# Local deformable attention: spread and write a step later, GpSimd's hat work on other steps, the first head's weights by three products and one sum

## The chip, the cores and the metric
The kernel runs on one core of a Trainium2 chip. The metric is the device time of one execution in microseconds (us), as a median over runs. The engines are TensorE (PE; its weight loads are shown as PEld), VectorE (DVE), ScalarE (ACT), GpSimd (POOL) and SyncE (SP), which issues most DMA transfers. Each works through its own queue in order.

## The reference
The program is a chain of four layers, each a token mixer and a feed-forward part, on x of (4, 64, 64, 128). The change touches the first mixer alone, a deformable attention with 4 heads of 32 channels and 9 taps (3x3, dilation 1, 3, 5, 7 for heads 0 to 3):

```python
qkv = conv2d(qkv.transpose(0, 3, 1, 2), w_dw, padding=1, groups=3 * c) + b_dw[None, :, None, None]
mask = jax.nn.sigmoid(conv1x1(pconv(q_img, pconv_mask_w), w_mask, b_mask))
for i in range(G):
    off = conv1x1(pconv(q_img, pconv_off_w[i]), w_off[i], b_off[i])
    dil = 2 * i + 1
    k_list.append(deform_sample(kv[0, :, i], off, mask, dil, dil * PAD))
    v_list.append(deform_sample(kv[1, :, i], off, mask, dil, dil * PAD))
...
attn = jax.nn.softmax(jnp.einsum('bgnc,bgckn->bgnk', qf, ks_), axis=-1)
out = jnp.einsum('bgnk,bgckn->bgnc', attn, vs_)
out = out.transpose(0, 2, 1, 3).reshape(b, h, w, c)
return out @ w_proj + b_proj
```

`deform_sample` reads the image at each tap moved by an offset, with bilinear weights between four pixels. Where no offset is over 1 in size, as with these inputs, a tap touches pixels of a small neighbourhood only.

## The kernel before, in words
`deformable_project` computes q, k, v, offsets and mask and leaves them in HBM. `deformable_near` is the local part, where the change lies. It works on 128 tiles of 128 pixels (two image rows); a tile's turn is a **step** T, and four tiles are a **chunk** c with the steps 4c to 4c+3. For each step:
- `products`: GpSimd copies the queries of the tile of the next step into qm (two buffers; L737).
- `product`: 64 TensorE matmuls (L766) give the products of the queries with whole runs of key pixels, in PSUM tiles S, one per head and one buffer each. `copy_products`: ScalarE copies them to `band` (L776). The next product can write S only after that.

For each chunk:
- `hats`, `rows_of_hats` and `hat_products`, all on GpSimd, make the bilinear weights: hat (L697 to L701), hy (L708 to L716), and H, four products for the four heads (L724).
- `attention`, on VectorE: shifts the bands by predicated copies (L785), multiplies them with H (L787), sums to the 9 logits (L794) and subtracts the maximum (L802 to L804).
- `spread`: the exponential on ScalarE (L810), its normalisation (L811 to L813), then the weight of each pixel of the neighbourhood, A, on VectorE: heads 1 to 3 by three products each (L817). Taps of head 0 overlap, so it has one product t0 (L823) and then three copies and additions per tap row (L827 to L830). `write`: four DMAs bring A to HBM (L835).

LAG steps after its product, each tile comes back. `read_dense` reads A in another layout into `dense` (L844), two steps ahead; `transpose` turns it on TensorE (L878), with copies dt to SBUF on ScalarE (L880); `weigh` multiplies it with values (L898; `value_block`, L856, loads them). After every fourth tile ScalarE copies the output to oT (L910, `values_done`), and a step later `projection` does the product with w_proj (L919), a ScalarE copy to o (L921) and two additions on GpSimd (L922, L923).

The order: the loop over T emits the work of a step; `step(T, first, do, 4)` emits `do(c)` at T = 4c + first. The blocks of TensorE (transpose, product, projection, weigh, in this order in a step) are chained by hand, `block`. GpSimd's hat work is tied by hand behind the qm copy of its step, `tc.issue_after(after[0].ins)`. All else is put into the queues by a planner at build time: it goes through the program with its own costs, and an engine that it finds free gets the earliest emitted instruction that it finds ready. Semaphores then keep data in order on the chip, whatever the times are.

Tile pools have a fixed number of buffers by tag: lg, m, me, H and band two; prod, hat, hy, t0, o and oT one; pt (for transposes and projection together) three.

Of the kernel before, what the change touches and what calls it, by code (L numbers as in the profile page):

```python
# [10 lines left out]
F32 = mybir.dt.float32  # L11
I32 = mybir.dt.int32
AF = mybir.ActivationFunctionType
ALU = mybir.AluOpType
AX = mybir.AxisListType
# [345 lines left out]
def window(ap, off, dims):  # L361

    return bass.AP(ap.tensor, ap.offset + off, [list(ap.ap[0])] + dims)
# [245 lines left out]
def deformable_near(k, dr, x, y, qd, kd, vd, od, masks, w_proj, b_proj):  # L609
# [19 lines left out]
    nc, tc = k.nc, k.tc  # L629
# [5 lines left out]
    with ExitStack() as ctx:  # L635
        wp = ctx.enter_context(tc.tile_pool(name="dn_w", bufs=1))
        sm = ctx.enter_context(tc.tile_pool(name="dn_s", bufs=2))
# [18 lines left out]
        for i in range(2):  # L656
            As.append([wp.tile([128, 4, WB[g], 4, 3], F32, tag=f"A{i}{g}", name=f"A{i}{g}") for g in range(4)])
            for t in As[i]:
                nc.vector.memset(t, 0.0)

        dd = [[dr.tile([128, 4 * PP[g] + 12], F32, tag=f"dd{i}{g}", name=f"dd{i}{g}") for g in range(4)] for i in range(3)]

# [14 lines left out]
        def behind():  # L677

            return tc.issue_after(last[0].ins) if last[0] is not None else ExitStack()

        def block(do, *args):

            with behind():
                last[0] = do(*args)
# [6 lines left out]
        def hats(c):  # L691

            of = ofs[c]
            hat = hat_of[c] = sm.tile([128, 8, 3, 4, 3, 3], F32, tag="hat", name="hat", bufs=1)
            src = window(of, 0, [[81, 4], [9, 8], [3, 3], [1, 3]])
            part = lambda i: window(hat, i, [[9, 4], [108, 8], [36, 3], [3, 3]])
            nc.gpsimd.tensor_scalar(part(0), src, -1.0, 0.0, op0=ALU.mult, op1=ALU.max)  # L697
            nc.gpsimd.tensor_scalar(part(2), src, 0.0, None, op0=ALU.max)
            flat = hat.rearrange("p s a t n i -> p (s a t n) i")
            nc.gpsimd.tensor_tensor(flat[:, :, 1], flat[:, :, 0], flat[:, :, 2], op=ALU.add)  # L700
            nc.gpsimd.tensor_scalar(flat[:, :, 1], flat[:, :, 1], -1.0, 1.0, op0=ALU.mult, op1=ALU.add)  # L701

        def rows_of_hats(c):

            of, hat = ofs.pop(c), hat_of[c]
            mk = sm.tile([128, 2, 36], F32, tag="mk", name="mk")
            at = lambda i: window(mk, 36 * i, [[0, 4], [1, 36], [0, 3]])
            nc.gpsimd.tensor_copy(mk[:, 0].rearrange("p (a t n) -> p a t n", a=3, t=4), window(of, 72, [[3, 3], [81, 4], [1, 3]]))  # L708
            nc.gpsimd.tensor_scalar(mk[:, 1], mk[:, 0], row, None, op0=ALU.mult)
            nc.gpsimd.tensor_tensor(mk[:, 0], mk[:, 0], mk[:, 1], op=ALU.subtract)  # L710
            hy = hat[:, 0:4].rearrange("p s a t n i -> p s (a t n) i")
            h4 = hy_of[c] = sm.tile([128, 4, 36, 4], F32, tag="hy", name="hy", bufs=1)
            nc.gpsimd.tensor_tensor(h4[:, :, :, 0:3], hy, at(0), op=ALU.mult)
            nc.gpsimd.tensor_tensor(hy, hy, at(1), op=ALU.mult)
            nc.gpsimd.tensor_tensor(h4[:, :, :, 1:3], h4[:, :, :, 1:3], hy[:, :, :, 0:2], op=ALU.add)
            nc.gpsimd.tensor_copy(h4[:, :, :, 3], hy[:, :, :, 2])  # L716

        def hat_products(c, groups):

            if 0 in groups:  # L720
                Hs[c] = sm.tile([128, 4, 36, 12], F32, tag="H", name="H")
            H, hat, h4 = Hs[c], hat_of[c], hy_of[c]
            for g in groups:
                nc.gpsimd.tensor_tensor(  # L724
                    H[:, g].rearrange("p n (a c) -> p n a c", a=4), window(h4, 144 * g, [[4, 36], [1, 4], [0, 3]]),
                    window(hat, 108 * (4 + g), [[3, 36], [0, 4], [1, 3]]), op=ALU.mult,
                )
# [79 lines left out]
        def spread(c):  # L807
            H = Hs.pop(c)
            lg, m, me, taps, wide, each = logits.pop(c)
            nc.scalar.activation(lg, lg, AF.Exp, scale=32 ** (-0.5))  # L810
            nc.vector.tensor_reduce(m, taps, axis=AX.XY, op=ALU.add)  # L811
            nc.vector.reciprocal(me, wide)
            nc.vector.tensor_tensor(lg, lg, each, op=ALU.mult)  # L813
            A = As[c % 2]
            for g in range(1, 4):
                for ty in range(3):
                    nc.vector.tensor_tensor(  # L817
                        window(A[g], ty, [[12 * DIL[g], 12], [3, 4], [12, 3]]), window(H, 432 * g + 144 * ty, [[12, 12], [3, 4], [1, 3]]),
                        window(lg, 36 * g + 12 * ty, [[1, 12], [0, 4], [0, 3]]), op=ALU.mult,
                    )  # L820

            t0 = sm.tile([128, 36, 12], F32, tag="t0", name="t0", bufs=1)
            nc.vector.tensor_tensor(t0, H[:, 0], window(lg, 0, [[1, 36], [0, 12]]), op=ALU.mult)  # L823
            for ty in range(3):
                a0 = lambda m0, n: window(A[0], 12 * m0 + ty, [[60, 4], [12, n], [3, 4]])
                tap = lambda tx, s0, n: window(t0, 144 * ty + 12 * tx + s0, [[36, 4], [1, n], [3, 4]])
                nc.vector.tensor_copy(a0(0, 3), tap(0, 0, 3))  # L827
                nc.vector.tensor_copy(a0(3, 2), tap(2, 1, 2))
                nc.vector.tensor_tensor(a0(1, 3), a0(1, 3), tap(1, 0, 3), op=ALU.add)
                nc.vector.tensor_tensor(a0(2, 1), a0(2, 1), tap(2, 0, 1), op=ALU.add)  # L830

        def write(c):
            for g in (1, 2, 3, 0):
# [82 lines left out]
        def projection(b, c, oT, xg):  # L916
            pr = ps.tile([128, 4, 128], F32, tag="pt", name="pr", bufs=3)
            for j in range(4):
                ins = nc.tensor.matmul(pr[:, j, :], oT[:, j, :], wpj, start=True, stop=True)  # L919
            o = sm.tile([128, 4, 128], F32, tag="o", name="o", bufs=1)  # L920
            nc.scalar.copy(o, pr)  # L921
            nc.gpsimd.tensor_tensor(o, o, bpj.to_broadcast([128, 4, 128]), op=ALU.add)  # L922
            nc.gpsimd.tensor_tensor(xg, xg, o, op=ALU.add)  # L923
            stores.append((now[0], b, c, xg))
            return ins

        def store(some):
            for o in some:
                _, b, c, xg = o
                nc.sync.dma_start(tokens(y, b, 4 * c, 4), xg)  # L930
                stores.remove(o)

        def step(T, first, do, every=1):
            n = T - first
            if 0 <= n < 128 and n % every == 0:
                do(n // every)

        LAG = 14
        for h in range(4):
            rows_of_keys(h)  # L940
        rows_of_queries(0)
# [1 line left out]
        offsets(1)  # L943
        products(0)
        hats(0)
        rows_of_hats(0)
        for T in range(128 + LAG):
            now[0] = T
            with behind():
                step(T, -1, products)  # L950
                step(T, -5, offsets, 4)
                with tc.issue_after(after[0].ins):
                    step(T, 0, lambda c: hat_products(c, (0, 1)), 4)
                    step(T, 1, lambda c: hat_products(c, (2, 3)), 4)
                    step(T, -2, hats, 4)
                    step(T, -1, rows_of_hats, 4)
                step(T, 4, attention, 4)
                step(T, 7, spread, 4)
                step(T, 9, write, 4)
                step(T, LAG - 2, read_dense)  # L960
                step(T, LAG, values)
            V, P = 0 <= T - LAG, T < 128
            late = [o for o in stores if o[0] <= T - 2]
            if V:
                block(transpose, T - LAG)
            if P:
                block(product, T)
            if project:
                block(projection, *project.pop())
            if V:  # L970
                block(weigh, T - LAG)
            with behind():
                store(late)
                step(T, 0, copy_products)
                step(T, LAG, values_done)
                if T % 4 == 1 and T < 124:
                    rows_of_queries(T // 4 + 1)
                if T < 96:
                    b, i = divmod(T, 32)
                    for h in range(4):  # L980
                        if i == min(8 * h + 13, 31):
                            rows_of_keys(4 * (b + 1) + h)
        if project:
            block(projection, *project.pop())
# [1637 lines left out]
```

## Time and profile before

| what | value |
|---|---|
| median of 3 runs | 7595.16 us (7589.31 to 7621.95) |
| profiled execution | 7610.45 us, its span 7608.4 us |
| PE busy over the span | 85% |
| DVE busy | 64% |
| ACT busy | 35% |
| POOL busy | 25% |
| mean granted PE clock | 0.895 |
| products of the local part (L766) | 678.8 to 1647.8 us |

The profile's columns: a group of instructions has its line, engine, operation, output and inputs by tile name, shapes and number. Busy time is the time in which an instruction of the group ran. An instruction's idle time is what its engine stood still before it; behind the arrow stands what ended that, as far as semaphores show. A wait for several semaphores is put down to the last. The granted clock is the share of full speed that TensorE's throttle allowed.

### The profile page before, as it was taken

To read this page: it belongs to the slowest core of one execution; us is meant where nothing else is said; L and a number is where in the kernel's file an instruction comes from. 1 tells how busy PE (TensorE), PEld (TensorE's weight loads), DVE (VectorE), ACT (ScalarE), POOL (GpSimd) and SP (SyncE) were. 2 spreads that over 40 slices of the span, in tenths; PEclk is the share of its full clock that TensorE was granted. 3 is DMA by queue.
4 is the path that set the end of the run, shared out by engine and by line. 5 is a ranking of instruction groups with operands and counts; after the bars stand their busy time and mean duration, and the time that the engine had idled before them with its cause. 6 is when DMAs were issued, how large, how long until landed. Compare 5 with 4: busy or idle time off the path is not lost. (4 is left out here: it accounts for less than half of the span.)

```text
span 7608.4 us, 157410 instructions
## 1 busy us (share of the span) xinstructions
PE 6501.1 (85%) x63791; PEld 3520.3 (46%) x63791; DVE 4893.8 (64%) x11051; ACT 2698.1 (35%) x6141; POOL 1932.7 (25%) x1794
## 2 busy tenths in 40 slices
PE   7996777875788789899989999798897997998989
PEld 3343666662455543355555555445225234242244
DVE  2213888865377546678855656674884876857877
ACT  3331333333154325411155665565004022041056
POOL 0003666640011100055522222253012112120135
PEclk9997888897789899999988889797997997988989
DMA  4436677772400031310000000001101111111101
GB/s 119 102 84 196 197 233 233 232 223 80 147 1 2 19 68 23 96 39 24 18 15 9 9 10 5 9 1 35 39 20 53 25 40 34 26 33 40 24 23 31
DMA packets 673787, 498.13 MB, mean 65 GB/s; under 512 B 296822, under 2 KB 588600, under 8 KB 669208
## 3 DMA queue, kind: packets, MB, share of 16 engines
q1 hardware_dynamic: 510158, 399.80, 18.8%
q10 hardware_dynamic: 162890, 88.11, 4.4%
q8 instruction: 509, 8.34, 0.5%
q14 instruction: 230, 1.88, 0.1%
HBM read 335.28 MB, written 152.33 MB: 64 GB/s over the span
## 5 line engine op out<-in xcount | busy, mean ns | idle before, releaser
L2491 DVE TENSOR_TENSOR t<-S,q 128x1536 f32<-128x1536 f32 (+3 forms) x608 | 1156.9, 1948 | 122.7 <-PE S L2479 117.5
L2479 PE MATMUL S<-R,L 32*128 32x512 f32 x4096 | 734.8, 651 | 90.0 <-DMA R<-wd 78.5
L2507 PE MATMUL acc<-t,sum 128*32 128x512 f32 x4096 | 639.6, 608 | 0.0
L766 PE MATMUL S<-kpad,qm 32*64 32x288 f32 (+3 forms) x8192 | 379.4, 408 | 191.1 <-ACT band L776 125.5
L2193 PE MATMUL pe<-ew,yT 128*128 128x512 f32 x1024 | 482.2, 606 | 26.2 <-DVE xs L2199 23.1
L785 DVE COPY_PREDICATED band<-bit,band 128x384 f32<-128x384 int32 (+11 forms) x384 | 382.6, 1102 | 175.6 <-ACT band L776 141.7
L1792 PE MATMUL acc<-w,attT 128*64 128x264 f32 x4096 | 485.4, 390 | 10.5 <-DMA xtl<-xtd 10.5
L2479 PEld LDWEIGHTS S<-R,L 32*128 32x128 f32 x4096 | 200.5, 186 | 611.1 <-issue 280.0
L2513 ACT COPY agg<-acc 128x512 f32<-128x512 f32 x32 | 18.8, 586 | 1196.7 <-DMA L<-pd 609.0
L1785 POOL TENSOR_TENSOR w<-xtl,ei 128x528 f32<-128x528 f32 x256 | 332.3, 1320 | 307.6 <-ACT ei L1784 202.9
L2199 DVE SCALAR_TENSOR_TENSOR xs<-pe,gate,xs 128x128 f32<-128x128 f32 x1024 | 332.5, 345 | 97.5 <-PE pe L2193 80.8
L766 PEld LDWEIGHTS S<-kpad,qm 32*64 32x64 f32 x8192 | 278.6, 151 | 245.4 <-issue 141.7
L1788 DVE TENSOR_TENSOR w<-xtl,pe 128x1056 f32<-128x1056 f32 x256 | 320.3, 1251 | 99.2 <-ACT ei L1784 89.0
L1792 PEld LDWEIGHTS acc<-w,attT 128*64 128x64 f32 x4096 | 283.6, 137 | 196.7 <-DVE w L1789 38.6
L2202 ACT ACTIVATE sc<-pe,gate 128x128 f32<-128x128 f32 x1024 | 291.3, 374 | 201.4 <-PE pe L2193 193.3
L2522 POOL TENSOR_TENSOR o<-o,bf 128x512 f32<-128x512 f32 x32 | 40.7, 1271 | 1231.1 <-ACT o L2521 1231.1
L514 PE MATMUL dw<-pad,diag 32*32 32x512 f32 x6912 | 308.4, 613 | 12.2 <-issue 6.1
L2507 PEld LDWEIGHTS acc<-t,sum 128*32 128x32 f32 x4096 | 92.8, 108 | 458.6 <-issue 436.2
L2193 PEld LDWEIGHTS pe<-ew,yT 128*128 128x128 f32 x1024 | 186.2, 194 | 233.5 <-issue 151.1
L880 ACT COPY dt<-pt 128x512 f32<-128x512 f32 x384 | 204.5, 604 | 165.6 <-PE pt L878 165.2
L878 PE MATMUL pt<-ident,D 128*128 128x128 f32 x1536 | 231.6, 304 | 17.5 <-DMA D<-dd 9.2
L1680 PE MATMUL acc<-y,xsp 128*64 128x512 f32 (+1 forms) x1088 | 237.1, 597 | 1.9 <-DVE xsp L1655 1.9
(525 smaller groups left out, 13001.1 us busy)
## 6 DMA issues: line engine op xcount, KB each, us to landing
vb<-vd SPq DMA_DIRECT2D x272, 256.0 KB
D<-dd SPq DMA_DIRECT2D x128, 192.0 KB
D<-dd SPq DMA_DIRECT2D x128, 168.0 KB
D<-dd SPq DMA_DIRECT2D x128, 144.0 KB
w<-in_e_weight_dram ACTq DMA_DIRECT2D x16, 1024.0 KB
w<-in_e_weight_dram SPq DMA_DIRECT2D x16, 1024.0 KB
wd<-s SPq DMA_DIRECT2D x32, 512.0 KB
D<-dd SPq DMA_DIRECT2D x128, 120.0 KB
```

The costliest lines, as they stand in the source:

```text
L514: nc.tensor.matmul(acc[g][32 * c : 32 * c + 32], diag[r, j, tap, :], pads[j][r, y0 : y0 + 8, tx : tx + 64], start=(tap == 0), stop=(tap == 8),
L766: ins = nc.tensor.matmul(acc[g][64 * h : 64 * h + 64].rearrange("p (a s) c -> p a s c", a=3), qm[rows, h, m, :], keys, start=(m == 0), sto ...
L785: nc.vector.copy_predicated(flat[:, :, 0:n], bit[:, 0, :, i : i + 1].to_broadcast([128, 48, n]), flat[:, :, s : s + n])
L1785: nc.gpsimd.tensor_tensor(w2[:, 2:4], xt[:, 2:4, 0:2], window(ei, 0, [[0, 2], [0, 2], [1, 132]]), op=ALU.mult)
L1788: nc.vector.tensor_tensor(w1, xt[:, :, 1:3], window(pe, 0, [[0, 4], [0, 2], [1, 132]]), op=ALU.mult)
L1792: nc.tensor.matmul(acc[b // 2][64 * (b % 2) : 64 * (b % 2) + 64], attT[:, b // 2, hp, 64 * (b % 2) : 64 * (b % 2) + 64], src[:, b].rearran ...
L2193: nc.tensor.matmul(pe[h].rearrange("p e c -> p (e c)"), yT[:, 128 * t : 128 * t + 128], ew[:, 4 * h : 4 * h + 4, :].rearrange("p e c -> p ...
L2199: nc.vector.scalar_tensor_tensor(xt, pe[0][:, e, :], gate[:, t, e : e + 1], xt, op0=ALU.mult, op1=ALU.add)
L2202: nc.scalar.activation(sc[:, e, j, :], pe[1][:, e, :], AF.Copy, scale=gate[:, t, 4 + e : 5 + e])
L2479: nc.tensor.matmul(S[:, j, :], Ls[n % 2][r, ag, :], Rs[n % 2][r, ag].rearrange("p x y -> p (x y)"), start=True, stop=True)
L2491: nc.vector.tensor_tensor(t[:, j0:j1].rearrange("p u (x y) -> p u x y", x=8), S[:, j0:j1].rearrange("p u (x y) -> p u x y", x=8), qf[:, q0 ...
L2507: nc.tensor.matmul(acc[0][32 * h : 32 * h + 32, :], sum4, t[:, j, :], start=(u < 4), stop=(u >= 60))
```

## The change
There are three edits.
1. The steps. `hat_products` for heads 0, 1 and 2, 3 go from first = 0 and 1 to 2 and 3, `hats` from -2 to -1, `rows_of_hats` from -1 to 0 (its first call moves from ahead of the loop into it), `spread` from 7 to 8, `write` from 9 to 10, and LAG from 14 to 15. `attention` stays at 4.
2. A of head 0. A tile `shared`, zeroed once, has for each tap row and tile 20 cells of 3 places; three products, one per tap column, each write to places of their own, and one sum over the 3 places gives A. This replaces t0 and the twelve small operations.
3. `o` uses oT's buffer.

```diff
+        shared = wp.tile([128, 720], F32, tag="shared", name="shared")
+        nc.vector.memset(shared, 0.0)
...
-            t0 = sm.tile([128, 36, 12], F32, tag="t0", name="t0", bufs=1)
-            nc.vector.tensor_tensor(t0, H[:, 0], window(lg, 0, [[1, 36], [0, 12]]), op=ALU.mult)
-            for ty in range(3):
-                a0 = lambda m0, n: window(A[0], 12 * m0 + ty, [[60, 4], [12, n], [3, 4]])
-                tap = lambda tx, s0, n: window(t0, 144 * ty + 12 * tx + s0, [[36, 4], [1, n], [3, 4]])
-                nc.vector.tensor_copy(a0(0, 3), tap(0, 0, 3))
-                nc.vector.tensor_copy(a0(3, 2), tap(2, 1, 2))
-                nc.vector.tensor_tensor(a0(1, 3), a0(1, 3), tap(1, 0, 3), op=ALU.add)
-                nc.vector.tensor_tensor(a0(2, 1), a0(2, 1), tap(2, 0, 1), op=ALU.add)
+            for tx in range(3):
+                nc.vector.tensor_tensor(
+                    window(shared, 13 * tx, [[60, 12], [3, 4], [12, 3]]), window(H, 12 * tx, [[36, 12], [3, 4], [1, 3]]),
+                    window(lg, tx, [[3, 12], [0, 4], [0, 3]]), op=ALU.mult,
+                )
+            nc.vector.tensor_reduce(
+                window(A[0], 0, [[1, 3], [60, 4], [3, 20]]), window(shared, 0, [[240, 3], [60, 4], [3, 20], [1, 3]]), axis=AX.X, op=ALU.add
+            )
...
-            o = sm.tile([128, 4, 128], F32, tag="o", name="o", bufs=1)
+            o = oT
...
-        LAG = 14
+        LAG = 15
...
         hats(0)
-        rows_of_hats(0)
...
-                    step(T, 0, lambda c: hat_products(c, (0, 1)), 4)
-                    step(T, 1, lambda c: hat_products(c, (2, 3)), 4)
-                    step(T, -2, hats, 4)
-                    step(T, -1, rows_of_hats, 4)
+                    step(T, 2, lambda c: hat_products(c, (0, 1)), 4)
+                    step(T, 3, lambda c: hat_products(c, (2, 3)), 4)
+                    step(T, -1, hats, 4)
+                    step(T, 0, rows_of_hats, 4)
                 step(T, 4, attention, 4)
-                step(T, 7, spread, 4)
-                step(T, 9, write, 4)
+                step(T, 8, spread, 4)
+                step(T, 10, write, 4)
```

## The prediction
> **What bounds the stage.** I read first the waits of the even part of the stage, attention 4 to attention 30 (819 to 1617 us): 26 groups of four steps in 798 us, 30.7 us each.
>
> ```profile
> 819.30:1617.30 798.00, 631.04 (x17922) 525.47 (x17921) 650.96 (x1379) 306.81 (x808) 526.94 (x652) 0.88 0.78 232
> ```
> ```profile
> ACT lg L810 <- DVE lg L804: 219.3, 26, 11.9
> ...
> DVE band L785 <- ACT band L776: 129.4, 26, 7.6
> ...
> PE S L766 <- ACT band L776: 72.3, 18, 7.1
> ```
>
> PE (631) and VectorE (651) are each busy four fifths, so neither is the bound. The waits form a ring: ScalarE stands 219 us before the exponential, TensorE waits for band copies behind it, and VectorE waits 129 us for the bands of the next group. The timeline of one turn (c = 10) shows the ring; the columns are start, length, engine, instruction, idle time before:
>
> ```profile
> 1002.59 5.03 DVE L785 COPY_PREDICATED band<-bit,band 128x384 f32<-128x384 int32 x6 [4.12 <-ACT band L776]
> 1002.64 2.75 POOL L724 TENSOR_TENSOR H<-hy,hat 128x432 f32<-128x432 f32 x2
> ...
> 1007.45 3.00 DVE L787 TENSOR_TENSOR prod<-band,H 128x144 f32<-128x144 f32 x6
> 1007.85 1.97 POOL L724 TENSOR_TENSOR H<-hy,hat 128x432 f32<-128x432 f32 x2
> ...
> 1008.69 1.56 ACT L880 COPY dt<-pt 128x512 f32<-128x512 f32 x3 [0.51 <-PE pt L878]
> ...
> 1014.59 1.63 PE L878 MATMUL pt<-ident,D 128*128 128x128 f32 x12
> 1016.36 1.49 DVE L787 TENSOR_TENSOR prod<-band,H 128x144 f32<-128x144 f32 x6
> ...
> 1020.88 0.32 ACT L810 ACTIVATE lg<-lg 128x144 f32<-128x144 f32 x1 [10.63 <-DVE lg L804]
> 1021.11 1.04 ACT L776 COPY band<-S 128x144 f32<-128x144 f32 x4
> ...
> 1021.52 4.82 PE L766 MATMUL S<-kpad,qm 32*64 32x144 f32 x64 [5.29 <-POOL hat L700]
> ...
> 1026.26 2.08 PE L919 MATMUL pr<-wpj,oT 128*128 128x128 f32 x8
> ...
> 1028.27 1.36 PEld L898 LDWEIGHTS out<-dt,vb 128*32 128x32 f32 x80 [0.23 <-issue]
> ...
> 1029.70 1.78 PE L878 MATMUL pt<-ident,D 128*128 128x128 f32 x12
> ...
> 1031.41 2.20 PE L766 MATMUL S<-kpad,qm 32*64 32x144 f32 x64
> ...
> 1033.97 0.60 DVE L785 COPY_PREDICATED band<-bit,band 128x384 f32<-128x384 int32 x1 [6.97 <-ACT band L776]
> ```
>
> Attention 10 begins when step 43's bands are copied. 18.29 us later the exponential runs, and only behind it the band copies of step 45. Then in a row: product 46 (begins 0.64 after the exponential and takes 4.74, at a granted clock of 0.50 over 1021.5 to 1026.3; product 44, at 1.00, took 2.2), projection 2.01, weighing 1.43, transposes 1.71, product 47 2.25, copy 0.31, together 31.38, and attention 11 starts. VectorE had its spread done by 1027.0 and idled 6.97.
>
> **The order is a planner's.** The code emits exponential 10 at the head of step 47, yet it stands in step 45, after that step's dt copies (1008.69) and before its band copies. From chunk 3 to 30 that place holds in every chunk. So work is queued where the planner, by its own durations, finds it ready; its place in the code only breaks ties. Moving `spread` from 7 to 8 and `write` from 9 to 10 therefore costs and gains nothing by itself: 0. What is tied by hand is GpSimd's work (behind the qm copies) and everything that LAG shifts: transposes, weighing and projection meet the product chunks one step later. So the projection leaves step 4c+6 for 4c+7, behind the product that attention c+1 needs, and falls between product 4c+3 and the transposes of 4c+4.
>
> This moves the planner's exponential as well. VectorE's attention starts at the same product; TensorE reaches the transposes of 4c+5 one projection later. Was there room for that? In the turn after this one all four writes of A are queued ahead of the four loads that the weighing of step 4c+5 releases:
>
> ```profile
> 1055.12 4.14 SPq L835 DMA_DIRECT2D dd<-A  x4
> ...
> 1059.36 3.23 SPq L856 DMA_DIRECT2D vb<-vd  x4
> ```
>
> The planner thus sees exponential and the whole spread (1020.88 to 1027.0, 6.1 us on the chip) end before a product and a weighing do (2.2 and 0.94 us at full clock). Its durations are not the chip's, but the exponential then sits early in product 4c+5, and a shift by a projection (1.16 to 2.08) likely puts it ahead of some dt copies of that step. That is the forecast's step, and its weakest.
>
> **The change, part by part,** in us per group.
> - A of the first head: out go the 128x432 product and twelve small operations, 1024.73 to 1027.0, 2.27. In come three 128x144 products at L817's pace (nine in 2.49, so 0.28 each, 0.83) and one sum of 720 elements: 1.95 for 1728 and 0.30 for 144 give 0.90. Gain 0.54 on VectorE, on the path 0: the 6.97 of idle time hide it. Without that cover it counts, 17 us in all. The memset of 720 elements, once, is below the 0.56 of those at L659: 0.
> - Projection off the path: L919 is 44.4 us in 32 groups, 1.39; gain 1.39. At its new place it delays the transposes of 4c+4, while attention still has 18 us to run: 0.
> - GpSimd: the hat products go from steps 4c and 4c+1 to 4c+2 and 4c+3, hats and rows one step on. The queue of GpSimd orders this against the qm copies: the copy for step 4c+5 now stands behind two hat products (1.19 each) and the hats (1.57+1.24+0.81+0.64), 6.6 us, and is needed two and a half steps (15 us) after the one before it: 0. The last two hat products end some 3 us before attention, and their first reader comes 13.8 us into it (1016.36): 0. Under attention, though, the company changes. Today four hat products run there; six L787 with two of them took 3.00, six without 1.49, so 0.75 each. Afterwards the first half meets the rows (L713, L714, L715) and, because the projection moved, both additions (L922, L923): five two-input operations, +0.75. Below: -0.75, if the rows slip behind the predicated copies. Above: +2.2, if two hat products meet the second half too. I take +0.75, from the nearest row.
> - The exponential ahead of the dt copies of step 4c+5: behind it now come the dt copies (1.56), the weighing of 4c+5 (0.94) and the transposes of 4c+6 (1.63) before product 4c+6 can start: +4.13; the wait of that product for the band copies (0.35) is then hidden: -0.35. Not below 0, since nothing is taken away; above, weighing and transposes run at half clock: +2.6.
> - `o` in `oT`'s buffer: the next oT copy waits for the additions, done at 1033.6; it comes at 1053.8. 20 us of cover, some 10 left when the additions come later: 0; without it at most their 2.6.
> - SyncE's queue: D reads have a step more between write and use; the stall on D is 3.7+3.6 us in 26 groups, gain at most 0.3, taken 0.
> - One step more at the end: the V-only step from 1669.02 to 1672.57 is 3.55 us, once. The first rows, now inside the loop, run under the first products: 0.
>
> Sum per group: 4.13 - 0.35 - 1.39 + 0.75 = 3.1. The 28 groups from the fourth on: 88, and 3.5 at the end: +91. The profiled execution took 7610.45 us (span 7608.4), 15.3 above the median of 7595.16. On the median: 7686, as a forecast 7685.
>
> **A rule against this change.** The row: with hat products beside them L787 took 0.75 more for each, while L794, a sum, is 1.95 whatever GpSimd does. The Trainium skill, SBUF — State Buffer, section "Who interferes with whom", says that VectorE instructions with two SBUF inputs and GpSimd's reads exclude each other for a whole instruction, and that sums never contend. By it the five operations would cost their full lengths (0.98+0.98+0.87+1.28+1.28) against four of 1.19, +0.6 in place of +0.75: the forecast by it is 4 us lower.
>
> **The rivals.**
> - B, the order on ScalarE stays (exponential after the dt copies). Then -1.39 + 0.75 = -0.6 per group, -18, and 3.5: 7581, between 7540 and 7625 with the ends of the GpSimd cost. For it: the planner's margin isn't in the profile. Against: the writes ahead of the loads. 0.30.
> - C, the other sign, as the change's name has it: the exponential slips behind the dt copies of step 4c+6. Behind it then stands one product in place of two; from there VectorE decides: 18.29 + 0.75 attention, 0.39, 1.2, 2.49, 1.73 are 24.9. DMA, 0.78 busy at 30.7, would stand at 0.96. I take 4 of the 5.8: -112+3.5: 7487, between 7440 and 7540. It decides from the point where attention, in the planner's time, lasts past the transposes of 4c+6; a projection inside attention speaks against it. 0.20.
> - D, the hat products come too late for attention 4c+4 (L787 waits for H): up to 5 per group, 7740. Against: 16 us of slack. 0.05.
>
> **Numbers.** About 0.5% (38 us) is what a measurement of this kernel can tell from no change. The forecast has 0.45, its own range 7640 (half of the 3.1 finds cover) to 7740 (1.7 more per group, two thirds of the half-clock cost). Faster: C and a part of B, 0.25. Same: most of B, a little of the forecast, 0.28. Slower: 0.47. The range 7490 to 7740 leaves out half of C and the upper ends.
>
> **What would show it.** Right: in ScalarE's order exponential c ahead of dt copies of step 4c+5, waits of L898 for dt, period near 33.8 us, the projection right after product 4c+3, L785 and L787 longer beside L922 and L923, L794 at 1.95, one sum near 0.9. Wrong: the exponential still after these dt copies (B), or one step on with VectorE's wait for bands nearly gone and DMA above 0.9 (C).

## The result, and the profile after

| | before | after |
|---|---|---|
| median (7 runs each) | 7595.16 us | 7649.96 us |
| lowest to highest | 7581.92 to 7621.95 | 7634.49 to 7671.82 |
| profiled execution, its span | 7610.45, 7608.4 | 7649.96, 7648.2 |
| local part, from the memset of kpad to the last weighing, in the profiles | 1048.9 us | 1120.1 us |
| a group of four steps, attention 4 to 30 | 30.69 us | 33.06 us |

The changed kernel is slower: ratio of the means 1.0068, 95% interval 1.0044 to 1.0091, some 52 us of the 7595. In the two profiles the local part is 71 us longer and the rest of the program, which the change doesn't touch, 31 us shorter. Over all fourteen profiles of this document that rest takes between 6520 and 6560 us, so a single pair of profiles doesn't tell the total; the period of the local part is read instead.

The waits from attention 4 to attention 30, the stretch that the prediction showed of before (first line: window, length, busy time and instructions of PE, PEld, VectorE, ScalarE, GpSimd, granted clock, DMA share, GB/s; below: who waits for whom, us in total, times, longest):

```profile
817.10:1676.60 859.50, 649.57 (x17882) 545.39 (x17882) 688.59 (x1144) 311.57 (x808) 561.27 (x650) 0.82 0.75 215
```
```profile
ACT lg L812 <- DVE lg L806: 268.4, 26, 13.4
POOL qm L739 <- issue: 236.0, 26, 10.9
...
DVE band L787 <- ACT band L778: 159.3, 28, 8.7
PE S L768 <- ACT band L778: 148.0, 26, 9.0
```

It is the ring of before, wound tighter: ScalarE's wait ahead of the exponential is 268 us (219 before), TensorE's for the band copies behind it 148 (72), VectorE's for the next bands 159 in 28 waits (129 in 26), and the granted clock is 0.82 (0.88). VectorE has fewer instructions (1144 for 1379) and is busy 38 us more. The timeline of one turn says why (start, length, engine, instruction, idle time before):

```profile
1010.96 4.45 DVE L787 COPY_PREDICATED band<-bit,band 128x384 f32<-128x384 int32 x6 [4.44 <-ACT band L778]
...
1015.27 2.25 DVE L789 TENSOR_TENSOR prod<-band,H 128x144 f32<-128x144 f32 x6
...
1015.97 1.14 POOL L715 TENSOR_TENSOR hy<-hat,mk 128x432 f32<-128x432 f32 x1
...
1017.44 9.95 DVE L787 COPY_PREDICATED band<-bit,band 128x768 f32<-128x768 int32 x6
...
1018.41 1.48 POOL L717 TENSOR_TENSOR hy<-hy,hat 128x288 f32<-128x288 f32 x1
...
1019.84 2.23 POOL L923 TENSOR_TENSOR oT<-oT,bpj 128x512 f32<-128x512 f32 x1
...
1023.12 2.21 POOL L924 TENSOR_TENSOR xg<-xg,oT 128x512 f32<-128x512 f32 x1
...
1027.24 3.02 DVE L789 TENSOR_TENSOR prod<-band,H 128x144 f32<-128x144 f32 x6
...
1027.89 1.97 POOL L726 TENSOR_TENSOR H<-hy,hat 128x432 f32<-128x432 f32 x2
...
1033.18 0.32 ACT L812 ACTIVATE lg<-lg 128x144 f32<-128x144 f32 x1 [9.32 <-DVE lg L806]
```

Three rows (two of them shown), both additions and two hat products lie under this attention; it takes 22.22 us where the turn of before that the prediction shows took 18.29. Both sides pay: the addition L923, 1.28 in the mean before, takes 2.23 here (mean 1.65), and the six larger predicated copies take 9.95. In that turn of before they took 6.20:

```profile
1010.37 6.20 DVE L785 COPY_PREDICATED band<-bit,band 128x768 f32<-128x768 int32 x6
```

The next table holds all kernels; each is described under the experiments. What it reads from each trace, in means over attentions 4 to 29: **att**, from the first predicated copy to the exponential; **excess**, how much longer the predicated copies and the products with H took than the shortest of the same shape in the trace of before, summed over one attention; **idle**, TensorE's standstill before product 4c+6 (the first behind the exponential); **p46**, that product; **gap**, from its end to product 4c+7 (with the projection in it where LAG is 14); **group**, from attention to attention; **local**, the local part as in the table above. Ratios are of the means of the runs, to before, run beside it. Where the exponential is tied later (exp_behind and exp_dt_adds), att includes its wait for that place, so there excess is the column to read. The group of a single trace is no sharper than some 0.3: spread_write_only, with the total of before, has 31.01 for 30.69.

| kernel | ratio [95%] | att | excess | idle | p46 | gap | group | local |
|---|---|---|---|---|---|---|---|---|
| before | 1 | 19.10 | 4.55 | 3.45 | 4.24 | 4.06 | 30.69 | 1048.9 |
| after | 1.0068 [1.0044, 1.0091] | 21.43 | 6.83 | 5.69 | 4.63 | 3.55 | 33.06 | 1120.1 |
| steps_only | 1.0080 [1.0060, 1.0100] | 20.40 | 5.82 | 5.21 | 4.63 | 4.74 | 32.97 | 1111.9 |
| lag_only | 1.0028 [1.0018, 1.0038] | 20.77 | 6.18 | 4.93 | 4.49 | 3.08 | 31.65 | 1075.6 |
| spread_write_only | 0.9997 [0.9981, 1.0012] | 19.18 | 4.59 | 3.81 | 4.29 | 4.12 | 31.01 | 1060.9 |
| sum_only | 1.0002 [0.9987, 1.0017] | 19.14 | 4.59 | 3.65 | 4.22 | 3.86 | 30.55 | 1046.7 |
| no_additions | 0.9999 [0.9985, 1.0013] | 18.78 | 4.00 | 1.57 | 3.67 | 3.42 | 30.00 | 1050.4 |
| warm | 1.0097 [1.0060, 1.0134] | 21.46 | 6.91 | 2.29 | 3.63 | 3.47 | 32.30 | 1103.1 |
| exp_ahead | 1.0202 [1.0180, 1.0223] | 21.55 | 6.89 | 0 | 2.46 | 3.23 | 35.70 | 1200.9 |
| exp_behind_5 | 0.9975 [0.9960, 0.9990] | 17.89 | 3.23 | 0 | 2.87 | 6.53 | 29.64 | 1030.3 |
| exp_behind_6 | 1.0007 [0.9991, 1.0023] | 19.42 | 2.80 | 0 | 2.71 | 6.86 | 30.63 | 1051.2 |
| adds_only | 1.0184 [1.0167, 1.0201] | 18.47 | 3.94 | 3.60 | 4.16 | 9.40 | 35.37 | 1183.3 |
| exp_behind_dt | 0.9969 [0.9956, 0.9982] | 19.39 | 3.52 | 0 | 2.58 | 5.91 | 29.49 | 1023.3 |
| exp_dt_adds | 0.9974 [0.9963, 0.9985] | 19.11 | 3.35 | 0 | 2.52 | 7.37 | 29.58 | 1019.1 |

ScalarE's order is the old one. In all 26 chunks the exponential of chunk c stands after the dt copies of step 4c+5 and before that step's band copies, in after as in before. So the predicted move of the exponential did not happen, and the loss is elsewhere: of the 2.37 us that a group got longer, attention has 2.33, product 4c+6 has 0.39, the gap behind it -0.51, the rest 0.16.

### The profile page after: what moved, and what is told of

It is laid out like the page before. It is cut to its first block, busy times and chain, and to the rows that moved or that the text cites. A ratio compares the mean times of both kernels' runs of the same rounds, so it can differ in the third digit from the quotient of the medians.

```text
span 7648.2 us, 157130 instructions
## 1 busy us (share of the span) xinstructions
PE 6498.0 (85%) x63791; PEld 3532.7 (46%) x63791; DVE 4931.3 (64%) x10764; ACT 2698.7 (35%) x6141; POOL 1969.2 (26%) x1794
## 5 line engine op out<-in xcount | busy, mean ns | idle before, releaser
L768 PE MATMUL S<-kpad,qm 32*64 32x240 f32 (+3 forms) x8192 | 400.1, 428 | 241.7 <-ACT band L778 196.4
L787 DVE COPY_PREDICATED band<-bit,band 128x384 f32<-128x384 int32 (+11 forms) x384 | 392.1, 1124 | 203.6 <-ACT band L778 165.4
L768 PEld LDWEIGHTS S<-kpad,qm 32*64 32x64 f32 x8192 | 297.6, 160 | 298.3 <-issue 251.0
L879 PE MATMUL pt<-ident,D 128*128 128x128 f32 x1536 | 249.2, 320 | 13.4 <-DMA D<-dd 6.0
```

Source lines behind the costliest of these rows:

```text
L768: ins = nc.tensor.matmul(acc[g][64 * h : 64 * h + 64].rearrange("p (a s) c -> p a s c", a=3), qm[rows, h, m, :], keys, start=(m == 0), sto ...
L787: nc.vector.copy_predicated(flat[:, :, 0:n], bit[:, 0, :, i : i + 1].to_broadcast([128, 48, n]), flat[:, :, s : s + n])
```

## The experiments

### The parts of the change, one at a time

**steps_only**: GpSimd's hat work on its new steps, all else as before.

```diff
-        rows_of_hats(0)
...
-                    step(T, 0, lambda c: hat_products(c, (0, 1)), 4)
-                    step(T, 1, lambda c: hat_products(c, (2, 3)), 4)
-                    step(T, -2, hats, 4)
-                    step(T, -1, rows_of_hats, 4)
+                    step(T, 2, lambda c: hat_products(c, (0, 1)), 4)
+                    step(T, 3, lambda c: hat_products(c, (2, 3)), 4)
+                    step(T, -1, hats, 4)
+                    step(T, 0, rows_of_hats, 4)
```

> The kernel before with GpSimd's hat work alone on its new steps (hat products at 2 and 3, hats at -1, rows at 0); LAG stays 14, spread 7, write 9. Theory 1 (GpSimd's two-input operations meet the predicated copies of attention): under attention now stand L713 to L715, two hat products and the second addition in place of four hat products, the difference of hat and the second addition, so attention goes from 19.1 to between 19.5 and 20.5 us and the program is 10 to 40 us slower than before. Theory 2 (the loss comes from LAG, by a longer standstill and a slower clock of TensorE): attention and total stay as before, within 10 us.

**lag_only**: LAG alone.

```diff
-        LAG = 14
+        LAG = 15
```

> The kernel before with LAG = 15 alone. Theory 1: both additions of the projection now meet attention beside the four hat products, 1.2 two-input operations more at 0.75 us, attention near 20.1 us; the projection leaves the path between the products of steps 4c+6 and 4c+7, so that gap falls from 4.06 to about 2.7; the sum is between -15 and +20 us. Theory 2: the gap stays near 3.5 because transposes and weighing run at half clock after a longer standstill, and the program is 30 us or more slower.

**spread_write_only**: the two steps that the planner can undo.

```diff
-                step(T, 7, spread, 4)
-                step(T, 9, write, 4)
+                step(T, 8, spread, 4)
+                step(T, 10, write, 4)
```

> The kernel before with spread at 8 and write at 10 alone. Theory 1: the exponential keeps its place in ScalarE's queue, ahead of the band copies of step 4c+5, and only the write of the first head moves in SyncE's queue: 0, within 10 us. Rival (the place in the code matters): the exponential stands a step later, period 25 to 28 us, 80 to 150 us faster.

**sum_only**: the first head's A by three products and one sum, and `o` in oT's buffer, as in the diff of the change.

> The kernel before with A of the first head by three products and one sum, and o in oT's buffer, alone. Theory 1: 0.5 us less work of VectorE per group, under the 5 to 7 us that it waits for the next bands: 0, within 10 us. Rival (VectorE is on the path): 17 us faster; or o in oT's buffer makes ScalarE wait for the additions: slower by up to 2.6 us per group, 80 us.

Measured: steps_only 7653.59 and lag_only 7620.29 us against 7597.71; spread_write_only and sum_only within their intervals of no change. The exponential stands in its old place in all four. So the loss belongs to the two edits that are tied by hand, and each of them lengthens attention. The loss of steps_only is larger than its expected 10 to 40 us, and lag_only, at 3.08 in the gap and some 21 us slower, lies between its two theories. The next table counts the two-input operations of GpSimd that run beside an attention's predicated copies and products with H, that is, after the first of these starts and before the last of them ends; what lies beside the sums behind them isn't counted. It has means over the same 26 attentions:

| per attention | before | after | steps_only | lag_only | no_additions |
|---|---|---|---|---|---|
| hat products | 3.77 | 1.85 | 2 | 4 | 0.85 |
| rows (hy, three operations) | 0 | 3 | 3 | 0 | 3 |
| additions | 0.85 | 2 | 1.38 | 2 | 0 |
| hat + hat (L700, L702) | 0.15 | 0.27 | 0.08 | 0.27 | 0.31 |
| all of them | 4.77 | 7.12 | 6.46 | 6.27 | 4.15 |
| excess, us | 4.55 | 6.83 | 5.82 | 6.18 | 4.00 |
| excess for each | 0.95 | 0.96 | 0.90 | 0.99 | 0.96 |

One price, 0.90 to 0.99 us for each operation, holds in all five traces, so the excess follows their number. A line fitted to all 364 attentions of the fourteen traces has 0.87 us for each operation and 0.44 with none of them. The two edits don't add up (61 and 21 us by the ratios, against 52); both push the same additions under attention. steps_only loses on the gap as well, 0.68: projection, weighing and transposes in it all take longer. The later LAG takes the projection out, and the gap goes from 4.74 to 3.55. Nothing here told of a planner that answered to the new steps.

### The additions taken away

**no_additions**: after, with the bias and the residual of the first mixer left out.

```diff
-            o = oT
-            nc.scalar.copy(o, pr)
-            nc.gpsimd.tensor_tensor(o, o, bpj.to_broadcast([128, 4, 128]), op=ALU.add)
-            nc.gpsimd.tensor_tensor(xg, xg, o, op=ALU.add)
+            nc.scalar.copy(xg, pr)
```

> The changed kernel without GpSimd's two additions after the projection (the output leaves out the bias and the residual x; the projection's product is copied straight to the store's tile). Theory 1 (two-input operations of GpSimd lengthen VectorE's instructions beside them): two of about seven under attention are gone, so attention goes from 21.4 to between 19.0 and 20.0 us, the period from 33.1 to about 31, the total about 7590. Theory 2 (a longer queue on GpSimd delays the qm copies and so the products): the same gain, but with attention at 21 and the products earlier.

Measured: 7595.1 us against 7596.16, so the whole loss is gone. Attention fell from 21.43 to 18.78, more than expected, its excess by 2.83. Not all of this is the additions themselves. In 15 of the 26 attentions the hat products now run behind the last product with H, beside the sums; the excess is 3.27 there and 5.01 in the 11 where both still run beside the products, 0.87 for each hat product. The 24 attentions of after with both hat products have 6.96, so the two additions took 1.95, about 1.0 each; the rest of the 2.83, some 0.9, is hat products that VectorE no longer meets. The same stretch of a turn, in the timeline, where the same six predicated copies took 9.95 above:

```profile
1014.89 7.82 DVE L787 COPY_PREDICATED band<-bit,band 128x768 f32<-128x768 int32 x6
...
1015.88 1.47 POOL L717 TENSOR_TENSOR hy<-hy,hat 128x288 f32<-128x288 f32 x1
...
1022.57 1.44 DVE L789 TENSOR_TENSOR prod<-band,H 128x144 f32<-128x144 f32 x6
...
1023.86 0.41 POOL L739 COPY qm<-q 128x64 f32<-128x64 f32 x2 [3.15 <-PE S L768]
...
1024.24 1.84 POOL L726 TENSOR_TENSOR H<-hy,hat 128x432 f32<-128x432 f32 x2
```

Here the six copies take 7.82. GpSimd is through with its queue early and waits 3.15 us for the product that frees qm, so VectorE's second products have no company and take 1.44 rather than 3.02. Idle and p46 fell too (5.69 to 1.57, 4.63 to 3.67): part of the recovered time is the clock. The group, 30.00, is even 0.69 below that of before, but from the start of attention 30 to the last weighing this kernel takes 113.2 us where before takes 98.3; why isn't shown.

### The standstill and the clock

**warm**: after, with 28 more transposes of the same data in step 4c+6, so that TensorE has work while attention goes on.

```diff
-                for g in range(4):
+                for g in [g for g in range(4) for _ in range(8 if (T + 15) % 4 == 2 and ty == 2 else 1)]:
```

> The changed kernel with the third transposes of the steps 4c+6 done eight times over into the same PSUM tile, 28 extra matmuls of 0.14 us, some 3.8 us, inside TensorE's standstill of 5.7 us ahead of product 4c+6. If the half clock after the standstill costs time, product 4c+6 falls from 4.6 to 2.5 to 3.5 us and the gap to the next product from 3.55 to about 2.7, the period by 1.5 to 3 us, the total by 40 to 85. If the clock plays no part: the same time, or slower by what of the 3.8 us does not fit.

Measured: the standstill before product 4c+6 fell from 5.69 to 2.29, the product from 4.63 to 3.63, the group by 0.76 and the local part by 17 us, while the median is 7657.39, and the ratio's interval holds the ratio of after. The expected 1.5 to 3 us per group and 40 to 85 us in all didn't come. By the trace's clock record TensorE had half clock for 307 of the 859.5 us from attention 4 to 30 in after (191 of 798 in before) and for 171 of 840 in warm. In the trace the half clock thus accounts for some 0.8 of the 2.37, net of what the added transposes cost; in the total it is not shown. What the clock does behind a long standstill, in after, stands in the timeline and in the windows of one turn (columns as in the first fence, the clock third from the right):

```profile
1067.38 4.82 PE L768 MATMUL S<-kpad,qm 32*64 32x144 f32 x64 [8.39 <-ACT band L778]
...
1072.13 1.51 PE L899 MATMUL out<-dt,vb 128*32 128x32 f32 x96
...
1073.57 2.83 PE L879 MATMUL pt<-ident,D 128*128 128x128 f32 x12
...
1076.33 2.57 PE L768 MATMUL S<-kpad,qm 32*64 32x144 f32 x64
```
```profile
1067.40:1072.10 4.70, 4.70 (x64) 3.63 (x64) 4.56 (x16) 2.09 (x6) 0.00 (x0) 0.50 0.75 231
1072.10:1073.60 1.50, 1.50 (x99) 1.41 (x97) 0.39 (x1) 1.07 (x4) 1.30 (x4) 0.50 1.07 282
1073.60:1076.30 2.70, 2.70 (x16) 2.40 (x12) 0.00 (x0) 1.76 (x3) 2.61 (x4) 0.50 0.76 211
1076.30:1078.80 2.50, 2.50 (x65) 1.97 (x64) 0.00 (x0) 0.59 (x1) 1.97 (x3) 0.83 0.83 232
```

After 8.39 us of standstill the half clock lasts 9.8 us (a mean of 0.83 over the last 2.50 is 0.85 more at half), through weighing (1.51, at full clock 0.94) and transposes (2.83, at full clock 1.63) as well. In this turn the longer attention is thus paid a second time, on the way to the next one.

### The exponential where the forecast had it, and later

**exp_ahead**: after, with the exponential tied ahead of the dt copies of step 4c+5.

```diff
-            nc.scalar.activation(lg, lg, AF.Exp, scale=32 ** (-0.5))
+            exped[c] = nc.scalar.activation(lg, lg, AF.Exp, scale=32 ** (-0.5))
...
-                nc.scalar.copy(dt, pt)
+                c, t = divmod(T + LAG - 5, 4)
+                with (tc.issue_after(exped[c].ins) if t == 0 and c in exped else ExitStack()):
+                    nc.scalar.copy(dt, pt)
...
-                step(T, 8, spread, 4)
+                step(T, 5, spread, 4)
```

> The changed kernel with the exponential of chunk c tied ahead of the dt copies of step 4c+5 in ScalarE's queue: the place that the forecast gave it and the planner did not. By the forecast's price (dt copies 1.56, weighing 0.94, transposes 1.63, less 0.35) the period is 3.8 us above that of the changed kernel (33.1), the total 7650 + 100, between 7710 and 7800. Rival: what comes behind the exponential finds cover under spread, and the total is within 20 us of 7650.

Measured: 7741.84 against 7589.61. The timeline has the forecast's chain: exponential, dt copies, weighing 4c+5 (after 8.21 of standstill), transposes, product 4c+6.

```profile
1030.03 0.32 ACT L813 ACTIVATE lg<-lg 128x144 f32<-128x144 f32 x1 [10.42 <-DVE lg L807]
1030.25 1.54 ACT L884 COPY dt<-pt 128x512 f32<-128x512 f32 x3
...
1031.36 1.78 PE L902 MATMUL out<-dt,vb 128*32 128x32 f32 x96 [8.21 <-ACT dt L884]
...
1033.07 2.83 PE L880 MATMUL pt<-ident,D 128*128 128x128 f32 x12
```

The group is 35.70, so 2.64 over after. The mechanism is real, and its price was taken at 3.78. Product 4c+6 begins 5.63 us behind the exponential instead of 0.64, but part of that comes back: now weighing and transposes run in the half-clock stretch and product 4c+6, at 2.46 rather than 4.63, no longer does.

**exp_behind_5**, **exp_behind_6**: before, with the exponential tied behind the band copies of step 4c+5 or 4c+6 (the second with `4 * c + 6`).

```diff
-                nc.scalar.copy(bands[c][g][:, :, t], acc[g].rearrange("p (a s) c -> p a s c", a=3))
+                copied[T] = nc.scalar.copy(bands[c][g][:, :, t], acc[g].rearrange("p (a s) c -> p a s c", a=3))
...
-            nc.scalar.activation(lg, lg, AF.Exp, scale=32 ** (-0.5))
+            with tc.issue_after(copied[min(4 * c + 5, 127)].ins):
+                nc.scalar.activation(lg, lg, AF.Exp, scale=32 ** (-0.5))
```

> The kernel before with the exponential of chunk c tied behind the band copies of step 4c+5 in ScalarE's queue, so that it stands a real step later; nothing else is changed. By the ring: one product instead of two stands behind the exponential, the period goes from 30.7 to between 25 and 28 us, where VectorE (attention 19 and spread 6) decides; the total is 75 to 160 us lower. Rival: the transfers (0.78 busy) or GpSimd's conflicts give it back: period 29 or more, less than 50 us.

> The same with the exponential behind the band copies of step 4c+6: no product waits behind it but that of 4c+7's copies, TensorE does not stand still for it, and VectorE alone decides: period 25 to 27 us, total 100 to 160 us lower. Rival: since TensorE runs ahead, more of GpSimd's work meets attention, which goes to 21 us or more, and the period is no shorter than with one step.

**exp_behind_dt**: before with sum_only's edit, and the exponential tied between the two, behind the dt copies of step 4c+6.

```diff
+            with (tc.issue_after(turned[4 * c + 6 - LAG].ins) if 4 * c + 6 >= LAG else ExitStack()):
+                nc.scalar.activation(lg, lg, AF.Exp, scale=32 ** (-0.5))
...
-                nc.scalar.copy(dt, pt)
+                turned[T] = nc.scalar.copy(dt, pt)
```

> The kernel before with the new sum, and the exponential tied behind the dt copies of step 4c+6, ahead of that step's band copies. In the run with the exponential behind the band copies of step 4c+5, projection and weighing waited for dt copies that stood behind the exponential (gap 6.5 us between the two products); here they stand ahead of it. VectorE then has hardly a wait left: period 27 to 28.5 us, 60 to 100 us faster than before. Rival: dense arrives too late (transposes wait for D) or more of GpSimd's work meets VectorE: period 29.5 or more, under 30 us.

Measured: 7578.73, 7598.29 (against 7596.16) and 7569.96 (against 7589.61). All three take the standstill before product 4c+6 away (idle 0), and the product then takes 2.6 to 2.9, but two of them gain some 20 us and one nothing. Where the rest of the gain went stands in the waits of exp_behind_dt, attention 4 to 30:

```profile
ACT dt L884 <- PE pt L882: 205.0, 131, 6.2
...
PEld pt L882 <- DMA D<-dd: 72.2, 90, 1.6
PE pt L882 <- DMA D<-dd: 68.2, 89, 2.5
...
DVE band L789 <- ACT band L780: 33.2, 15, 5.4
```

VectorE hardly waits for bands any more (33 us for 129 in before) and is busy 683 of 767. The transposes now wait for D: 72 us on the loads' side, where before had 3.6; in the gap alone TensorE stands 1.53 per group, before 0.04. Whether slower transfers or their later issue make D late isn't shown, and no run has the later LAG beside this order. The exponential now stands behind dt copies that wait for these transposes, so VectorE waits 42 us for it, four times the 10.1 of after:

```profile
DVE m L816 <- ACT lg L815: 42.2, 26, 8.6
```

And the spread met GpSimd instead. First the shared products of after, then those of exp_behind_dt with the sum behind them, both from the timeline:

```profile
1004.64 0.95 DVE L825 TENSOR_TENSOR shared<-H,lg 128x144 f32<-128x144 f32 x3
```
```profile
1032.47 3.44 DVE L828 TENSOR_TENSOR shared<-H,lg 128x144 f32<-128x144 f32 x3
...
1033.49 0.86 POOL L719 TENSOR_TENSOR hy<-hy,hat 128x288 f32<-128x288 f32 x1
...
1034.30 1.34 POOL L926 TENSOR_TENSOR oT<-oT,bpj 128x512 f32<-128x512 f32 x1
...
1035.94 0.90 DVE L832 TENSOR_REDUCE A<-shared 128x240 f32<-128x720 f32 x1
```

Three products of 144 took 3.44 beside rows and an addition, 0.95 without; the sum of 720 takes 0.90 either way (0.90 in the mean of after too). exp_behind_6 has yet more of the D waits (84 us). exp_behind_5 and exp_behind_dt thus came out as their rivals had it, with groups of 29.64 and 29.49. exp_behind_6 fits neither of its theories: no gain, and yet the lowest excess of all.

### The additions on TensorE

**adds_only**: before with sum_only's edit, and bias and residual added by products into the projection's PSUM tile. **exp_dt_adds**: the same edit on exp_behind_dt.

```diff
-                ins = nc.tensor.matmul(pr[:, j, :], oT[:, j, :], wpj, start=True, stop=True)
-            o = oT
-            nc.scalar.copy(o, pr)
-            nc.gpsimd.tensor_tensor(o, o, bpj.to_broadcast([128, 4, 128]), op=ALU.add)
-            nc.gpsimd.tensor_tensor(xg, xg, o, op=ALU.add)
+                nc.tensor.matmul(pr[:, j, :], oT[:, j, :], wpj, start=True, stop=False)
+                nc.tensor.matmul(pr[:, j, :], k.ident, xg[:, j, :], start=False, stop=False)
+                ins = nc.tensor.matmul(pr[:, j, :], k.ones_row, bpj[0:1, 0, :], start=False, stop=True)
+            nc.scalar.copy(xg, pr)
```

> The kernel before with the new sum for the first head, and bias and residual added on TensorE (a product of the identity with x and one of ones with the bias, into the projection's PSUM tile) in place of GpSimd's two additions. Attention loses the 0.85 additions that meet it, 1.2 us: near 17.9. But the projection, on the path here, is longer by some 1.5 to 2.5 us. Expected: between 15 us faster and 30 us slower than before. Rival (the additions do not matter to attention here): attention stays at 19.1, 40 to 60 us slower.

> The same, and the two additions on TensorE as well. With VectorE the bound, the additions beside its instructions cost 1.4 us each where they meet, so the period falls by a further 1 to 2.5 us, to 25.5 to 27 us; 90 to 150 us faster than before. Rival: TensorE's longer projection takes it back: no faster than without.

Measured: 7733.39 and 7572.05, against 7589.61. In adds_only attention fell by 0.63, half of what was expected, and the loss is far above both forecasts, because the twelve products (two records each) stand in the gap, on the path between product 4c+6 and the next attention: 6.11 us in the mean where the projection took 1.30, and the gap is 9.40 in place of 4.06. The window of one such stretch shows them at half clock throughout:

```profile
1037.20:1044.70 7.50, 7.50 (x28) 5.71 (x27) 1.16 (x3) 1.07 (x4) 4.38 (x9) 0.50 0.82 234
```

Where the standstill is gone (exp_dt_adds) they cost the gap 1.5, and the total can't be told from exp_behind_dt, as its rival said. The lowest ratio is that of exp_behind_dt, 0.9969 [0.9956, 0.9982] of before; the intervals of exp_dt_adds and exp_behind_5 overlap it.

## Why the prediction was right, and where it was not

The direction and the size were met, 7650 in a forecast of 7685 with its own range of 7640 to 7740, but not for the forecast's reason. In its sum, +3.1 per group, the largest term did not occur, and other terms cost more than taken. What was measured is +2.37. That the total still came out near is luck: 3.78 that was priced and did not come is offset, but for 0.77, by 1.58 more in attention (2.33 for 0.75), 0.88 less gain from the projection (0.51 for 1.39), and 0.39 in product 4c+6 and 0.16 in the rest, which the sum had at nothing.

- **The exponential ahead of the dt copies, +4.13 - 0.35**: measured 0. This step failed, as the weakest link that the prediction called it. The inference from the writes queued ahead of the loads was wrong: the planner's place held in all 26 chunks, which is rival B's condition. exp_ahead shows that the step itself was sound where the place is forced, at 2.64 for 3.78.
- **GpSimd under attention, +0.75**: measured +2.28 of excess, +2.33 in attention. This mis-sized term carries the result, and mostly by its count. The prediction took five two-input operations for four; measured are 7.12 for 4.77: three rows, two additions and nearly two hat products in after, while before already had 0.85 additions. The prediction named hat products in the second half as its upper end (+2.2), and that end is what came. In the mean they begin 15.3 us into an attention of after, and its second products with H end at 18.5. In no_additions they begin at 15.0, hardly earlier, but the second products end at 15.6, because the predicated copies ahead of them end at 13.7 and not at 16.2. So it is mostly the longer copies that bring the products under the hat products. The price was off less: some 0.9 for each operation in place of 0.75, and about 1.0 for an addition.
- **The rule weighed against it.** no_additions takes about 1.0 us off VectorE for each addition of 1.28, a hat product costs 0.87 with a shortest length of 0.93, and spread's three products grew from 0.95 to 3.44 beside rows. The Trainium skill, SBUF — State Buffer, section "Who interferes with whom", has one of the two block the other for a whole instruction; the hat products and the unmoved sums (1.95 and 0.90) are near it, while an addition costs less than its whole length.
- **Projection off the path, -1.39**: in the gap -0.51. By TensorE's instructions in it, the projection's 1.30 left the gap as the step said, but weighing went from 1.09 to 1.32 and the transposes from 1.69 to 2.24, and product 4c+6 ahead of it from 4.24 to 4.63: TensorE has half clock for more of the time, 307 of 859.5 us where before had 191 of 798. The prediction had the half clock as an end of the exponential's cost only, not as a cost of any longer attention.
- **A of the first head, `o` in oT, spread and write a step later**: 0 each, as predicted and as sum_only and spread_write_only show. Three products took 0.95 (0.83 predicted), the sum 0.90 (0.90).
- **One step more at the end, +3.55**: from the start of attention 30 to the end it is 106.3 for 98.3; two longer groups are 4.7 of these 8.0, which leaves 3.3. This end differs by 2.5 us between traces of equal totals (98.3 in before, 100.8 in sum_only), so the agreement says little.
- **Rival B** had the order right and the total wrong, 7581 with 7625 as its end: it took the GpSimd term at 0.75 as well. At the measured 2.33 its own sum is +0.9 per group; what product, weighing and transposes took longer (0.39 + 0.23 + 0.55) brings it to 2.1 of the 2.37.
- **Rival C**: exp_behind_5 and exp_behind_dt make a later exponential happen. It gains some 20 us, not 112. In exp_behind_dt VectorE did become nearly the bound, as the rival said, but its busy time had grown beside GpSimd's work, and D arrives late.
- **Rival D** (attention waiting for H): among after's waits VectorE has none for H.

The signs that the prediction named told the cases apart: order (B), period 33.06 for 33.8, L787 and L789 longer beside L923 and L924, L796 at 1.95. The period alone would have confirmed the wrong cause.

## What to carry to other kernels

When work of GpSimd moves to another step, list all its two-input operations that will lie under VectorE's two-input work and predicated copies, here at some 0.9 us for each operation of 288 to 512 elements; those that the stage itself reaches once it has become longer belong to the list. A longer stage also lengthens TensorE's standstill, and the half clock behind it can be a second bill. Check the order in the queue before pricing what stands behind a moved instruction, and tie an order that matters by hand: one such line gained 0.3% (exp_behind_dt, beside the new sum, which alone gains nothing), where the whole change lost 0.7%.

## What the runs showed of the hardware that was not expected

- The slowing goes both ways: beside predicated copies GpSimd's additions of 512 take 1.65 and 1.71 in the mean, up to 2.25, for 1.28 and 1.34 before; its rows up to 1.53 for 0.88.
- A small copy on GpSimd can stand long among predicated copies: two qm copies of 64 elements, 0.42 when alone, took 3.54 in exp_behind_dt (1016.87, under the six L789 of 768 and more); the longest single ones took 7.47 in no_additions (at 988.57) and 7.36 in before. These two started under a run of predicated copies and ended only with the last product with H, while the predicated copies beside them kept to 1.01 to 1.29.
- The half clock lasted 9.8 us after a standstill of 8.39, with TensorE at work nearly throughout; after one of 7.58 (product at 1001.42) it ended within 4.4. The Trainium skill, TensorE: Matmul & The Clock Gate, in Part 1, has some 3.4 us of work bring the full clock back; the second case is near that and the first is not. The length of the standstill doesn't tell the two apart: in after the half clock lasted 7.6 us in the mean past the start of product 4c+6 for standstills under 5 us and 7.5 for longer ones (the 8 and 16 groups whose product began at half clock).
